# Products of ones, earlier matrix groups and later scoring in the graph layer of a graph-and-experts kernel

## The chip, the cores and the metric

The kernel runs on one NeuronCore of a Trainium2 chip. The core has five engines, each with its own queue that is worked off in order: TensorE (PE, matrix products and transposes), VectorE (DVE), ScalarE (ACT), GpSimd (POOL) and SyncE (SP, which here only starts transfers). Sixteen DMA engines move data between DRAM and the on-chip memory. The metric is the device time of one execution in microseconds (us).

## The reference

The input is x (1024 rows of 512, float32) and a list of 16384 edges sorted by their destination. Two layers follow:

```
h  = layernorm(x) @ W                      # 1024x512 @ 512x512
x  = x + relu(segment_sum(edge_weight * h[dst], src) + bias)
t  = layernorm(layernorm(x))               # two norms before the experts
scores = sigmoid(layernorm(x) @ Wg.T + bg) # 64 experts, the best 2 of each row
y  = sum over the 2 experts of weight * (silu(t W1' + b1') * (t W3' + b3')) @ W2 + b2
x  = x + y + shared_expert(t)
```

The graph layer's gather and sum over edges can be written as a product of a 1024x1024 matrix A (the summed edge weights) with h. The kernel does that.

## The kernel before

All of it is float32 with some bf16 helpers. A row tile is 128 rows, so there are NT = 8 tiles.

**Start (lines 219 to 331).** VectorE waits for the first edge of each partition (`first`, line 261), compares it with thresholds (`below`, 263), and TensorE counts the results in two small products (266). From the count VectorE gets the rows of the edge list that hold the block boundaries (268, 270), POOL loads them (273), and VectorE finds where each block of destinations starts (319 to 324). POOL then loads the windows of edges (331): destination, source and weight, and behind them on its queue the bias rows (`base_d`, 335), the small weights (`ws_raw`, 341, 342, and others) and the zeroing of `y_d` (372), whose source row is written by a memset on VectorE (371).

**Products with W.** `center(i)` is VectorE's mean of a tile and its subtraction. `turn_h(i)` is four transposes on TensorE (193) and a copy on ScalarE (300). `times_w(i)` is four products with W (307, each shown as two records) and a scaled copy on ScalarE (308) into `hws`. The order of these calls is written out by hand: TensorE, VectorE, ScalarE and POOL issue in the order of the program, except that some instructions behind the branch `tc.If(unsure)` (446) are placed ahead of it.

**Edge parts.** VectorE splits the loaded windows into parts (381 to 388). TensorE transposes the six parts (393 to 395), which stand behind `times_w(3)`, and VectorE copies the results (396, 399).

**One-hots and matrix groups.** The matrix A is made in two halves (h = 0, 1) of 8 groups each; I number the groups 0 to 15. `one_hots(h, g)` (401 to 421) is four steps on VectorE (408 three times, 419) and a cast on ScalarE (417). `matrix_group` (489 to 500) is 16 small products on TensorE (495) and two copies on ScalarE (500) into A. The one-hots run two groups ahead of the products. All groups stand behind `times_w(7)`. In the second half, each group is followed by `turn` (four transposes, 507, and a copy to AT, 508) and one or two products with h (`weighted_sum`, 514); by the end of the second half the first half's sums of tiles 0, 1 and 2 are done ahead (`NE3 = 3`).

**Tile loop (689 to 718).** In pass t the remaining products of tile t are run, `turn` is done for tile t + 2, and then four more steps stand one, two or three passes behind: `store_nx(t-1)` (ScalarE 545, POOL 546), `score_bias`, `turn_x` and `scores` of tile t-1 (TensorE 558, 193, 563; ScalarE 552, 566, 567), `choose`, `rank`, `put` and `slots` of tile t-2 (VectorE 572 to 611, TensorE 597, 599, POOL 620, 622) and `listed(t-3)` (TensorE 628). `finish(t)` closes the pass: VectorE adds the bias rows and x (529, 530), takes the norms (166, 167, 174 to 183) and writes the normalized row tile (187) and the shift (541).

The rows of one pass as they stand in the code:

```
for a in todo[:n0]: weighted_sum(*a)
turn(As[1], 1, t + 2); summed(t + 1); store_nx(t - 1); listed(t - 3)
for a in todo[n0:n1]: weighted_sum(*a)
score_bias(t - 1); turn_x(t - 1)
choose(t - 2); rank(t - 2); put(t - 2); slots(t - 2, ...)
for a in todo[n1:]: weighted_sum(*a)
scores(t - 1); finish(t)
```

**Experts (721 on).** From the lists (720) POOL gathers the rows of a pair of experts (752), TensorE transposes them (193) and multiplies them with the weights (781, 803), and POOL scatters the results (810). SyncE loads the weights of all 64 experts through two rings of 13 buffers; most of the graph layer's tiles are taken from the same rings.

## Time and profile before

| what | us |
|---|---|
| median of 4 runs (445.25 to 448.84) | 446.4 |
| profiled execution | 446.28 |
| its span, first to last instruction | 444.5 |
| first product with W starts | 9.94 |
| edge parts on TensorE start | 30.48 |
| matrix group 0 starts | 46.74 |
| first sum done, `finish(0)` starts | 92.08 |
| first gather of rows for an expert | 174.42 |

Busy time in the span: TensorE 394.3 us (89%), VectorE 244.0 (55%), ScalarE 117.3 (26%), GpSimd 121.9 (27%). A busy TensorE is not TensorE at its peak: its records overlap, and the clock that the throttle grants falls below 1.00 in some stretches. A row of the timeline gives start and duration in us, engine, line of the kernel, operation, output<-input, and a count; in brackets stands how long the engine was idle before it and what released it. Matrix products of float32 show as two records each.

### The profile page before, as it was taken

What the parts mean: (1) busy time and instruction counts of PE and PEld (TensorE: products, weight loads), DVE (VectorE), ACT (ScalarE), POOL (GpSimd) and SP (SyncE); (2) the same over time, 40 slices, a digit from 0 to 9 for tenths busy, and PEclk for the clock granted to TensorE, in tenths of its full rate; (3) what the DMA queues carried; (4) which work ended last, traced back from release to release, by engine and by line L of the source; (5) the groups of instructions that cost most, each with busy time, mean ns of one, the idle gap of its engine ahead of it and who ended that gap; (6) DMA issues with size and microseconds to landing.
All of it is one profiled execution on the core that took longest, in us unless ns stands there. A gap on an engine that the chain in (4) does not pass through costs nothing.

```text
span 444.5 us, 6426 instructions
## 1 busy us (share of the span) xinstructions
PE 394.3 (89%) x2130; PEld 186.9 (42%) x2130; DVE 244.0 (55%) x723; ACT 117.3 (26%) x241; POOL 121.9 (27%) x162
## 2 busy tenths in 40 slices
PE   2999769988999963799976999999999999999793
PEld 1554446645555542334422343444434434434241
DVE  4969899648777883422366353534424333331781
ACT  1235799432222221111201121221221212212100
POOL 5450800002333234232231141423231322313000
PEclk9999999988999975799998999999999999999898
DMA  8377492992534199379999999999999999999572
GB/s 261 99 112 104 126 358 103 406 375 67 171 119 160 51 383 370 124 233 414 407 406 407 408 408 406 408 409 408 405 409 408 406 408 406 406 409 375 220 279 89
DMA packets 40983, 132.50 MB, mean 298 GB/s; under 512 B 7116, under 2 KB 7260, under 8 KB 40816
## 3 DMA queue, kind: packets, MB, share of 16 engines
q1 hardware_dynamic: 31040, 109.66, 63.1%
q0 software_dynamic: 9184, 20.28, 15.7%
q10 hardware_dynamic: 720, 2.10, 1.2%
q8 instruction: 18, 0.29, 0.3%
q14 instruction: 21, 0.17, 0.1%
HBM read 124.13 MB, written 18.62 MB: 321 GB/s over the span
## 4 chain that ended last, share of the span: by engine, by line
PE 69%; DVE 8%; DMA 5%; ACT 4%; issue 2%; POOL 0%; POOLq 0%; ACTq 0%; DVEq 0%
PE xph L781 23%; PE xpy L803 12%; PE acc L514 12%; PE xpt L193 3%; DMA y_d<-xy,lists 3%; PE xph L777 2%; PE xpht L793 2%; ACT ov L417 2%; PE ph L495 2%; PE xpy L942 2%; PE ph L563 2%; PE pt L507 1%; PE pt L193 1%; DMA bw<-w_d,lists 1%; ACT A L500 1%
## 5 line engine op out<-in xcount | busy, mean ns | idle before, releaser
L781 PE MATMUL xph<-w,xT 128*64 128x512 f32 (+1 forms) x520 | 121.5, 596 | 0.1
L810 POOL DMA_INDIRECT y_d<-xy,lists x30 | 31.1, 1037 | 146.0 <-DMA y_d<-xy,lists 68.6
L803 PE MATMUL xpy<-w,xhT 128*64 128x512 f32 (+1 forms) x260 | 66.5, 614 | 4.7 <-ACT xhT L795 4.7
L781 PEld LDWEIGHTS xph<-w,xT 128*64 128x64 f32 (+1 forms) x520 | 38.6, 138 | 61.3 <-issue 57.6
L514 PE MATMUL acc<-hw,AT 128*128 128x512 f32 x128 | 62.5, 615 | 0.4 <-ACT AT L508 0.4
L786 DVE TENSOR_TENSOR xh<-xa,xph 128x256 f32<-128x256 f32 x33 | 13.9, 421 | 86.8 <-ACT xa L784 72.6
L784 ACT ACTIVATE xa<-xph 128x256 f32<-128x256 f32 x33 | 12.7, 385 | 114.8 <-PE xph L781 114.8
L752 POOL DMA_INDIRECT rows<-nx_d,tokens x32 | 34.7, 1083 | 15.7 <-issue 8.0
L803 PEld LDWEIGHTS xpy<-w,xhT 128*64 128x64 f32 (+1 forms) x260 | 19.7, 143 | 45.4 <-issue 38.3
L764 DVE TENSOR_TENSOR xT<-xpt,gT 128x512 f32<-128x512 f32 x32 | 22.1, 690 | 25.1 <-PE xpt L193 23.1
L806 ACT COPY xy<-xpy 128x512 f32<-128x512 f32 x33 | 19.4, 587 | 48.4 <-PE xpy L803 42.8
L307 PE MATMUL ph<-w_sb,hT 128*128 128x512 f32 x64 | 31.5, 640 | 0.7 <-ACT hT L300 0.7
L514 PEld LDWEIGHTS acc<-hw,AT 128*128 128x128 f32 x128 | 22.6, 195 | 17.3 <-issue 16.7
L193 PE MATMUL xpt<-ident,rows 128*128 128x128 f32 x132 | 22.0, 293 | 4.8 <-DMA rows<-nx_d,tokens 4.8
L546 POOL DMA_DIRECT2D nx_d<-row x8 | 4.5, 563 | 76.8 <-ACT row L545 76.8
L417 ACT CAST ov<-eq 128x1536 f32<-128x1536 bf16 x16 | 24.8, 1553 | 0.0
L766 DVE TENSOR_TENSOR xT<-xT,bT 128x512 f32<-128x512 f32 x32 | 22.1, 692 | 1.1
L495 PE MATMUL ph<-ov,ol 128*32 128x128 f32 x512 | 17.4, 276 | 5.4 <-ACT A L500 5.0
L193 PEld LDWEIGHTS xpt<-ident,rows 128*128 128x128 f32 x132 | 19.2, 211 | 5.0 <-DMA rows<-nx_d,tokens 4.9
L793 PEld LDWEIGHTS xpht<-ident,xh 128*128 128x128 f32 x66 | 11.7, 210 | 19.7 <-DVE xh L786 10.7
L193 PE MATMUL pt<-ident,row 128*128 128x128 f32 x64 | 12.4, 322 | 8.3 <-DVE row L187 2.8
L793 PE MATMUL xpht<-ident,xh 128*128 128x128 f32 x66 | 14.7, 305 | 4.9 <-DVE xh L786 4.9
(271 smaller groups left out, 505.7 us busy)
## 6 DMA issues: line engine op xcount, KB each, us to landing
w<-in_L_ffn_W_dram SPq DMA_DIRECT2D x195, 512.0 KB
y_d<-row POOLq DMA_DIRECT2D x1, 4096.0 KB
ys<-y_d SPq DMA_DIRECT2D x8, 512.0 KB
base_d<-in_L_gnn_bias_dram POOLq DMA_DIRECT2D x1, 2048.0 KB
row<-base_d POOLq DMA_DIRECT2D x8, 256.0 KB
nx_d<-row POOLq DMA_DIRECT2D x8, 256.0 KB
w_sb<-in_L_gnn_W_dram ACTq DMA_DIRECT2D x1, 1024.0 KB
res<-in_x_dram SPq DMA_DIRECT2D x2, 512.0 KB
```

Source lines behind the costliest of these rows:

```text
L193: nc.tensor.transpose(ps[:, k, :], v[:, k, :], ident[:n, :n])
L307: nc.tensor.matmul(ph, hT[:, k, :], w_sb[:, k, :], start=(k == 0), stop=(k == KC - 1))
L417: nc.scalar.copy(ov[:, :, :VA], eq)
L495: nc.tensor.matmul(pa[LO * w:LO * (w + 1), u, :], ol[:, q, :], ov[:, q, :], start=True, stop=True)
L514: nc.tensor.matmul(accs[t], ATs[h][t // 4][:, t % 4, wq, :], hws[h][:, wq, :], start=(h == 0 and wq == 0), stop=(h == NH - 1 and wq == NQ ...
L752: nc.gpsimd.indirect_dma_start(out=rows, out_offset=None, in_=nx_d[:, :], in_offset=bass.IndirectOffsetOnAxis(ap=of, axis=0), bounds_check ...
L764: nc.vector.tensor_tensor(xT.rearrange(view, n=n), pt.rearrange(view, n=n), g[:, :, :, None].to_broadcast(over), ALU.mult)
L766: nc.vector.tensor_tensor(xT.rearrange(view, n=n), xT.rearrange(view, n=n), b[:, :, :, None].to_broadcast(over), ALU.add)
L781: nc.tensor.matmul(ph[n * r:(n + 1) * r], xT[:, k, n * r:(n + 1) * r], w13[:, :, k, :], start=False, stop=(k == KC - 1))
L793: nc.tensor.transpose(pt[:, c, :], v[:, c, :], ident)
L803: nc.tensor.matmul(py[n * r:(n + 1) * r], hT[:, c, n * r:(n + 1) * r], w2[:, c, :], start=(c == 0), stop=(c == HC - 1))
L810: nc.gpsimd.indirect_dma_start(out=y_d[:, :], out_offset=bass.IndirectOffsetOnAxis(ap=numbers, axis=0), in_=y, in_offset=None, bounds_chec ...
```

## The change

It has three parts.

1. **Products of ones.** A helper `keep_warm(n)` multiplies the bf16 tile `ones_b` with itself into an accumulator that nobody reads. Nine such products stand ahead of the two counting products, six behind them, and two behind `turn_h(0)`.
2. **Groups among the products with W.** Three of the sixteen matrix groups are moved ahead of the branch: group 0 behind `times_w(5)`, group 1 behind `times_w(6)`, group 2 behind `times_w(7)`. Their one-hots move up with them, from where on one-hots run one group ahead instead of two. The transposes of the edge parts move into the middle of `times_w(3)`. The zero row is written by ScalarE instead of VectorE. The count of edges inside the windows (`sm`, `inside`) moves behind the one-hots of group 1.
3. **Scoring of the first three tiles.** Tile 0 is scored in pass 2 instead of pass 1, tiles 1 and 2 both in pass 3 (before: passes 2 and 3). The choice follows one pass later (tile 0 in pass 3, tiles 1 and 2 in pass 4), the lists again one pass later (pass 4, and both in pass 5). From tile 3 on nothing changes. The rings of `so` and `bo` have 6 buffers instead of 4.

```diff
+            def keep_warm(n):
+                pz = psc.tile([P, D], F32, name="acc")
+                for _ in range(n):
+                    nc.tensor.matmul(pz, ones_b, ones_b[:, None, :].to_broadcast([P, D // P, P]), start=True, stop=True)
...
+            keep_warm(9)
             pn = psh.tile([P, D], F32, name="ph")
             for h in range(NH):
                 nc.tensor.matmul(pn[:, h:h + 1], below[:, h, :], ones_b[:, 0:1], start=True, stop=True)
+            keep_warm(6)
...
             for k in range(KC):
+                if k == KC // 2 and amid:
+                    amid()
                 nc.tensor.matmul(ph, hT[:, k, :], w_sb[:, k, :], start=(k == 0), stop=(k == KC - 1))
...
             turn_h(0)
+            keep_warm(2)
...
-            nc.vector.memset(zero, 0.0)
+            nc.scalar.activation(zero, ones[:, 0:1].to_broadcast([P, D]), AF.Copy, scale=0.0)
...
             turn_h(4)
-            times_w(3)
...
+            times_w(3, turn_parts)
...
             turn_h(5)
+            ohs[0] = one_hots(0, 0)
             times_w(4)
             turn_h(6)
-            times_w(5)
+            ohs[1] = one_hots(0, 1)
...
+            times_w(5)
+            matrix_group(As[0], 0, 0, ohs.pop(0))
...
             turn_h(7)
+            ohs[2] = one_hots(0, 2)
             times_w(6)
+            matrix_group(As[0], 0, 1, ohs.pop(1))
+            ohs[3] = one_hots(0, 3)
             times_w(7)
+            matrix_group(As[0], 0, 2, ohs.pop(2))
...
-                    so = rt.tile([P, P], F32, name="so", bufs=4)
+                    so = rt.tile([P, P], F32, name="so", bufs=6)
...
-            for g in range(8):
-                ohs.append(one_hots(0, g + 2) if g + 2 < 8 else one_hots(1, g + 2 - 8))
-                matrix_group(As[0], 0, g, ohs.pop(0))
-                if g == 1:
+            for g in range(3, 8):
+                ohs[g + 1] = one_hots(0, g + 1) if g + 1 < 8 else one_hots(1, 0)
+                matrix_group(As[0], 0, g, ohs.pop(g))
+                if g == 3:
...
-                if have(3):
-                    listed(t - 3)
+                scored, chosen, put_down = (
+                    ([], [0], [1, 2])[t - n] if n <= t < n + 3 else [t - n] if have(n) else [] for n in (1, 2, 3))
+                for c in put_down:
+                    listed(c)
+                if len(scored) == 2:
+                    score_bias(scored[0])
+                    turn_x(scored[0])
                 for a in todo[n0:n1]:
                     weighted_sum(*a)
-                if have(1):
-                    score_bias(t - 1)
-                    turn_x(t - 1)
-                if have(2):
-                    choose(t - 2)
-                    rank(t - 2)
-                    put(t - 2)
-                    slots(t - 2, nc.vector if t - 2 == NT - 1 else nc.gpsimd)
+                if len(scored) == 2:
+                    scores(scored.pop(0))
+                for c in scored:
+                    score_bias(c)
+                    turn_x(c)
+                for c in chosen:
+                    choose(c)
+                    rank(c)
+                    put(c)
+                    slots(c, nc.vector if c == NT - 1 else nc.gpsimd)
                 for a in todo[n1:]:
                     weighted_sum(*a)
-                if have(1):
-                    scores(t - 1)
+                for c in scored:
+                    scores(c)
```

The scaling of the shared expert's weights (636, VectorE) keeps its place by group: it stood behind the one-hots of group 3 and now stands behind those of group 4.

## The prediction

> **What bounds the kernel now.** I read the page's busy line first, then the chain of waits, then the timelines of TensorE, VectorE and ScalarE in the first 145 us, where all edits lie. TensorE is busy for 394.3 of 444.5 us. Behind 145 us every step hangs on the lists made from the scores, and the weight loads wait for buffers that the same steps free, so I count time won before 145 us as time won at the end.

> The early stage, from the timeline (start, duration, engine, line, what, count, in brackets idle time before and its releaser):

> ```profile
> 9.94 6.31 PE L307 MATMUL ph<-w_sb,hT 128*128 128x512 f32 x8 [0.68 <-ACT hT L300]
> 19.23 3.60 PE L307 MATMUL ph<-w_sb,hT 128*128 128x512 f32 x8
> 27.04 3.60 PE L307 MATMUL ph<-w_sb,hT 128*128 128x512 f32 x8
> 30.48 0.27 PE L393 MATMUL acc<-ident,windows 128*128 128x128 f32 x1
> 51.27 1.08 PE L495 MATMUL ph<-ov,ol 128*32 128x128 f32 x32 [0.84 <-ACT A L500]
> 63.16 1.08 PE L495 MATMUL ph<-ov,ol 128*32 128x128 f32 x32
> ```
> ```profile
> 24.93 0.48 DVE L371 MEMSET row<- 128x512 f32 x1
> 31.22 1.22 DVE L396 CAST values<-acc 128x1024 bf16<-128x1024 f32 x1 [3.21 <-PE acc L394]
> 44.74 0.43 DVE L636 TENSOR_TENSOR wall<-ws_raw,gs_sb 128x256 f32<-128x256 f32 x1 [0.26 <-DMA ws_raw<-in_L_ffn_Ws_dram]
> ```

> The first product with W takes 6.31 us, the later ones 3.60: TensorE starts slowly. VectorE waits 3.21 us for the transposed edge parts, which stand behind times_w(3). From 51.27 a matrix group comes every 1.92 us, paced by ScalarE (cast 1.37 plus copies 0.55); from 63.16 TensorE itself paces.

> The tile loop, from the timelines, and granted clock by stretch (columns: stretch, length, busy time of PE, PEld, DVE, ACT, POOL, granted clock, DMA share, GB/s):

> ```profile
> 92.08 0.69 DVE L529 TENSOR_TENSOR row<-row,acc 128x512 f32<-128x512 f32 x1 [6.79 <-PE acc L514]
> 97.35 0.15 DVE L541 SCALAR_TENSOR_TENSOR mrs<-mvr,rs 128x1 f32<-128x1 f32 x1
> ```
> ```profile
> 97.58 1.10 PE L193 MATMUL pt<-ident,row 128*128 128x128 f32 x4 [2.11 <-DVE mrs L541]
> 105.89 0.72 PE L193 MATMUL pt<-ident,row 128*128 128x128 f32 x4 [1.03 <-issue]
> 107.23 0.19 PE L597 MATMUL ph<-chosen,before_b 128*128 128x64 bf16 x1 [0.62 <-ACT hT L552]
> ```
> ```profile
> 97.60:100.40 2.80, 2.80 (x8) 1.74 (x8) 0.00 (x0) 2.42 (x3) 1.08 (x2) 0.50 0.95 376
> 107.20:110.70 3.50, 3.47 (x11) 2.47 (x12) 2.79 (x11) 0.03 (x1) 2.24 (x5) 0.53 0.23 80
> ```

> finish(0) holds VectorE from 92.08 to 97.50 (5.42 us), and TensorE waits 2.11 us for its row, then 1.03 and 0.62. After such waits it runs at a clock of 0.50 for about 3 us.

> **Part 1, products of ones.** 17 bf16 products of 128x512. No row has one; the bf16 products at 117.88 and 117.91 (64 columns) start 0.03 us apart, so I take 8 x 0.03 = 0.24 us at full clock, 0.48 at half. The bound above is a whole f32 record of the same width when cold, 6.31/8 = 0.79; below, L777 starts two in 0.24, 0.12 each. Nine from 1.15 (ones_b written) end at 5.5, when the start search's products are due. Six after them end at 7.2 to 8.6; turn_h(0) stands at 8.16 now, so up to 0.5 is lost if they run slowly. Two lie beside the 0.59 us copy of hT. At 0.79 the nine would end at 8.3 and hold back L268 and all VectorE behind it by 2.7 us, of which its idle 0.41 and 1.33 cover 1.7: then 1 us is lost.
> If they warm the clock, times_w(0) falls from 6.31 to about 3.4 and ends by 13.4. ScalarE must then wait for rsx (VectorE, 14.36) before copying hw(0), then hT(1), wall, gT (0.69+0.58+0.37+0.37); turn_h(2) follows at 16.4 and times_w(1) at 17.0 instead of 19.23: 2.2 won there. Half a warm-up gives the same, since 14.36 ends last.
> [...]

> **Part 2, three groups earlier.** The memset leaves VectorE (0.40 to the next start) for ScalarE, which idles 2.5 us there; the nearest row, L1010, costs 0.56 each. Its user, the zeroing DMA on POOL, stays behind base_d's landing. VectorE's parts thus end at 27.6, not 28.0. TensorE has half of times_w(3) done at 26.7, turns the parts by 27.9 and finishes them plus the second half (1.72) at 29.7, against 31.13 now. The cast L396 starts at 28.0 instead of 31.22.
> From 29.7 TensorE needs: turn_h(5) to (7) and times_w(4) to (7), 3 x 0.57 + 4 x 3.43, three groups at 1.03 and the count's 0.14, 18.7 in all: 48.5, and 0.4 for the branch as now (the idle at 47.96): group 3 at 48.9 instead of 51.27. The casts of groups 3 and 4 stand before the branch on ScalarE, so group 4 follows at once, and from group 3's copies on (50.0) five steps of 1.92 lead to group 9 (the second half's second) at 59.7, against 63.16. The wait of 0.41 for the first AT behind it is gone too: group 10 starts at 62.3 instead of 66.36. I take **4.0 us**.
> VectorE's cover: its groups 0 to 4 end at 43.1, then it waits for ws_raw, which landed at 44.74, since base_d's load, ahead of it in POOL's queue, is not moved. Behind that come the branch (0.7) and 11 groups at 2.54: it ends at 73.7, not 76.5, and its cast input for group 9 at 56.8, 1.4 us before ScalarE wants it. If that cover goes, each us beyond 1.4 is lost.

> **Part 3, scoring later.** Everything 4.0 earlier, finish(0) runs 88.1 to 93.5. Tiles 1 and 2 need few products (1.72 + 0.45 + 1.72 before tile 1 is summed, at 91.8), so VectorE does finish(1) to 98.9 and finish(2) to 104.3 without pause. TensorE goes on with tile 2, score_bias(0) and turn_x(0) and is at scores(0) at 96.6. But ScalarE issues store_nx(1) before the copy of hT(0), and store_nx(1) needs finish(1): 98.9 + 0.75 + 0.59 = 100.3. **New wait: 3.7 us**; queued behind it are tile 3's products.
> Then scores 0.9 and pass 3 with two tiles (8 products 6.9, turn 0.45, twice bias, turn, scores 0.4+0.57+0.9, rank 0.05): 112.3. Pass 4 reaches rank(1) 7.2 later, 119.5. rank(2) follows it in TensorE's queue, but choose(2) stands behind put(1) on VectorE: 1.1 + 1.35 us: **second wait, 2.6 us**, with four products and scores(3) behind it. Pass 5 starts at 124.8 and, with one more pair of list products (0.38), ends at 135.1 against 140.40 now. At full clock that is 5.3 us won, 1.3 of it by this part.
> Both waits are as long as or longer than the 2.11 us after which 2.8 us ran at 0.50. I charge 1.4 each, **2.8**. Bounds: 0 to 1.75 each by the rows above (3.5 at 0.53), more if the low clock lasts on. DMA order, row buffers and the wider rings of so and bo cost nothing: base rows load 10 us ahead, and POOL's 2.35 us per tile for the two tiles ends at 126, before the lists at 129.
> [...]

> **Sum.** 4.0 + 1.3 - 2.8 = 2.5. The profiled execution took 446.28 (span 444.5 and 1.8 around it), 0.1 below the median of 446.4. Forecast **443.8 us**.

> **Rivals.**
> A. The clock stays up through the waits: 2.8 comes back, gain 5.3, **441.0**. For: 51 to 59 us ran at 1.00 with TensorE 56% busy. Against: both rows at half clock.
> B. The ones don't warm the clock (the change doesn't do what it says): times_w(0) stays at 6.31, the parts are turned at 29.4 and all behind is 1.7 later: gain 0.8, **445.5**. For: the first 6 us of work are slow now. Against: 3.8 us or more of added work.
> C. Slower: the low clock after the two waits. The new waits sum to 6.3 us, against 3.8 removed. If each is followed by two stretches of 3.5 us at half clock, it costs 2 x 3.5 = 7.0, not 2.8: 446.3 + 1.7 = **448.0**. It turns the sign where the clock's loss passes 5.3. Against: each stretch ended after 2.8 to 3.5 us.
> D. The front's gain is lost on the way, because the expert loop doesn't start earlier (its first weights come late): 446.3. Against: TensorE's first wait there is for gathered rows, not weights.

> **How the numbers follow.** Forecast 0.46, A 0.24, B 0.14, C 0.10, D 0.06. 1% is 4.5 us, about what a measurement of this kernel can tell from no change. Faster by more holds A and a part of the forecast, where less than 0.8 is lost to the clock: 0.27. Slower by over 1% needs C in an extreme form or something unseen: 0.08. The range reaches from under A (441.0, less 1 for an earlier end of the waits) to between B and C: 440.0 to 447.2.

> **What would show it.** Right: the second product with W near 17 us, the cast of L396 at about 28, group 10 at 62 to 63; a wait of 3 to 4 us before the first score products and of 2 to 3 us before the second rank of pass 4, both followed by a granted clock near 0.5; the gather of the first rows 2 to 3 us before 174.42. Wrong: a times_w(0) still over 6 us, those waits missing, or an expert loop of another length than now.

## The result: 0.4% slower

The changed kernel takes 447.93 us (median of 52 executions, 443.65 to 449.79), the kernel before 445.71 (78 executions, 442.48 to 449.95). The ratio is 1.0039, with a 95% interval of 1.0026 to 1.0051: 1.2 to 2.3 us slower. (The ratio is an estimate of its own; the quotient of the two medians is 1.0050.) The forecast was 443.8, its range ended at 447.2. The profiled execution of the changed kernel took 450.12 us (span 448.4), 2.2 over its median and above the highest of the 52, so it is a late one of its kind.

TensorE's timeline in the first 65 us of the changed kernel:

```profile
1.21 4.02 PE L224 MATMUL acc<-ones_b 128*128 128x512 bf16 x9 [1.21 <-DVE ones_b L123]
9.76 3.70 PE L317 MATMUL ph<-w_sb,hT 128*128 128x512 f32 x8 [0.24 <-ACT hT L308]
16.14 1.23 PE L193 MATMUL pt<-ident,raw 64*128 64x64 f32 x8 [1.59 <-ACT hT L308]
18.27 4.43 PE L317 MATMUL ph<-w_sb,hT 128*128 128x512 f32 x8
26.90 1.88 PE L317 MATMUL ph<-w_sb,hT 128*128 128x512 f32 x4
28.62 0.27 PE L405 MATMUL acc<-ident,windows 128*128 128x128 f32 x1
50.27 1.96 PE L443 MATMUL ph<-ov,ol 128*32 128x128 f32 x64 [0.33 <-PEq L480]
61.15 1.08 PE L443 MATMUL ph<-ov,ol 128*32 128x128 f32 x32 [0.19 <-ACT ov L431]
```

The ones do speed up the first products with W: times_w(0) lasts 3.70 instead of 6.31. It does so in all ten profiles with the ones that follow, and takes 5.35 to 6.63 in the four without. But TensorE is then ahead of ScalarE, waits 1.59 us for a copy, and times_w(1) behind it takes 4.43 instead of 3.60. The parts are turned from 28.62 (before 30.48; the forecast had them done by 27.9), group 3 runs at 50.27 (before 51.27, forecast 48.9), group 9 at 61.15 (63.16, 59.7).

VectorE's timeline:

```profile
29.37 1.23 DVE L410 CAST values<-acc 128x1024 bf16<-128x1024 f32 x1 [1.45 <-PE acc L406]
89.38 0.69 DVE L550 TENSOR_TENSOR row<-row,acc 128x512 f32<-128x512 f32 x1 [7.27 <-PE acc L535]
94.73 0.68 DVE L550 TENSOR_TENSOR row<-row,acc 128x512 f32<-128x512 f32 x1
100.07 0.68 DVE L550 TENSOR_TENSOR row<-row,acc 128x512 f32<-128x512 f32 x1
```

finish(0), (1) and (2) follow each other without pause, as forecast, and finish(0) starts 2.7 us earlier than before (92.08). The two new waits of the tile loop, on TensorE, and what ScalarE does ahead of the first:

```profile
101.52 1.81 PE L584 MATMUL ph<-wall,hT 128*128 128x128 f32 x8 [3.32 <-ACT hT L573]
125.44 0.20 PE L618 MATMUL ph<-chosen,before_b 128*128 128x64 bf16 x1 [2.50 <-DVE chosen L600]
```
```profile
100.19 0.81 ACT L566 ACTIVATE row<-res,mrs,rs 128x512 f32<-128x512 f32 x1 [3.95 <-DVE mrs L562]
100.91 0.56 ACT L573 COPY hT<-pt 128x512 f32<-128x512 f32 x1
```

Both waits are there, at the places forecast and nearly as long: 3.32 (3.7) and 2.50 (2.6). ScalarE stands at the store of tile 1's row (L566) for 3.95 us, and the copy of hT(0) behind it. By finish(7), at 158.41 against 158.59, of the 2.7 us that finish(0) had won 0.2 are left.

### The profile page after: what moved, and what is told of

It reads as the page before. It is cut to its first block, busy times and chain, and to the rows that moved or that the text cites. A ratio compares the mean times of both kernels' runs of the same rounds, so it can differ in the third digit from the quotient of the medians.

```text
span 448.4 us, 6462 instructions
## 1 busy us (share of the span) xinstructions
PE 400.8 (89%) x2147; PEld 188.1 (42%) x2147; DVE 243.6 (54%) x722; ACT 117.5 (26%) x242; POOL 120.8 (27%) x162
## 4 chain that ended last, share of the span: by engine, by line
PE 54%; DMA 17%; DVE 9%; issue 4%; ACT 3%; POOL 0%; POOLq 0%; ACTq 0%; DVEq 0%
PE xph L809 15%; DMA y_d<-xy,lists 14%; PE acc L535 11%; PE xpy L831 9%; PE xpt L193 2%; PE ph L584 2%; PE ph L443 2%; PE pt L528 2%; PE xpht L821 2%; DMA y_d<-xy,lists_o 1%; PE xph L805 1%; PE pt L193 1%; ACT ov L431 1%; PE xpy L937 1%; DMA bw<-w_d,lists 1%
## 5 line engine op out<-in xcount | busy, mean ns | idle before, releaser
L831 PE MATMUL xpy<-w,xhT 128*64 128x512 f32 (+1 forms) x260 | 67.5, 622 | 4.8 <-ACT xhT L823 4.8
L317 PE MATMUL ph<-w_sb,hT 128*128 128x512 f32 x64 | 30.0, 609 | 0.2 <-ACT hT L308 0.2
L193 PE MATMUL xpt<-ident,rows 128*128 128x128 f32 x132 | 22.0, 293 | 5.0 <-DMA rows<-nx_d,tokens 5.0
L193 PEld LDWEIGHTS xpt<-ident,rows 128*128 128x128 f32 x132 | 19.3, 211 | 5.1 <-DMA rows<-nx_d,tokens 5.1
L443 PEld LDWEIGHTS ph<-ov,ol 128*32 128x32 f32 x512 | 13.1, 109 | 12.6 <-ACT ov L431 6.7
```

The costliest lines, as they stand in the source:

```text
L193: nc.tensor.transpose(ps[:, k, :], v[:, k, :], ident[:n, :n])
L317: nc.tensor.matmul(ph, hT[:, k, :], w_sb[:, k, :], start=(k == 0), stop=(k == KC - 1))
L443: nc.tensor.matmul(pa[LO * w:LO * (w + 1), u, :], ol[:, q, :], ov[:, q, :], start=True, stop=True)
L831: nc.tensor.matmul(py[n * r:(n + 1) * r], hT[:, c, n * r:(n + 1) * r], w2[:, c, :], start=(c == 0), stop=(c == HC - 1))
```

## The experiments

One quantity carries most of what follows: the tile loop from the start of finish(0) to the start of finish(7). It is 66.5 us in the profile before and 69.0 in the changed kernel. A "low stretch" is a stretch at a granted clock of 0.50. Every one that I measured in steps of 0.1 us is 3.4 us long, or a multiple of it, so by estimate one costs 1.7 us of TensorE's work (half of 3.4; a run below takes two of them away and wins 3.4).

| kernel | finish(0) | loop | low stretches in the loop | median us | ratio to before (95%) |
|---|---|---|---|---|---|
| before | 92.08 | 66.5 | 2 | 445.71 | |
| before, second profile | 91.83 | 65.3 | 1 | | |
| changed | 89.38 | 69.0 | 2 | 447.93 | 1.0039 (1.0026 to 1.0051) |
| part 1 alone | 90.60 | 63.7 | 1 | 445.86 | 1.001 (0.998 to 1.004) |
| part 2 alone | 90.99 | 65.3 | 1 | 445.27 | 0.9998 (0.9969 to 1.0027) |
| part 3 alone | 92.60 | 69.0 | 2 | 449.82 | 1.0109 (1.0073 to 1.0145) |
| parts 1 and 2 | 89.53 | 64.6 | 1 | 444.18 | 0.995 (0.992 to 0.998) |
| changed, ones in the two waits | 90.15 | 65.7 | 0 | 445.74 | 0.9996 (0.9972 to 1.0019) |
| changed, first wait gone | 89.83 | 65.1 | 1 | 443.14 | 0.994 (0.992 to 0.997) |
| changed, second wait gone | 89.25 | 65.6 | 1 | 445.05 | 0.9955 (0.992 to 0.999) |
| changed, both waits gone | 88.23 | 61.7 | 0 | 442.07 | 0.990 (0.986 to 0.993) |
| parts 1 and 2, ones ahead of the rows | 88.40 | 64.7 | 1 | 442.51 | 0.991 (0.9885 to 0.994) |
| both waits gone, ones ahead of the rows | 89.51 | 61.7 | 0 | 439.75 | 0.985 (0.981 to 0.9885) |
| the same and ones in the front's wait | 88.62 | 61.7 | 0 | 439.04 | 0.985 (0.9815 to 0.988) |

The first three numbers of a row are from one profiled execution each; the medians and ratios are from 5 to 78 executions, each ratio against executions of the kernel before on the same chip.

### The parts alone

Part 1 alone (only the three calls of `keep_warm`):

> The kernel before with part 1 alone (the products of ones). My theory after reading the changed kernel's trace: the ones warm the clock (times_w(0) lasts 3.7 us instead of 6.31), but TensorE then waits 1.6 us for ScalarE and falls to half clock, so that the end of times_w(1) comes only 0.1 us earlier (22.7 instead of 22.8); part 1 is worth 0 to 0.2 us, ratio 0.999 to 1.000. Rival, the prediction's own count: 2.2 us won at times_w(1) and carried to the end, ratio 0.995.

times_w(1) starts at 17.8 (before 19.2, in its second profile 19.0), and finish(0) 1.2 to 1.5 us earlier, in a profile that has no low stretch in the front. The time doesn't move. Nine profiles here have the ones and nothing in TensorE's wait behind them, which is 1.48 to 1.95 us long in eight of them and 0.51 in one. In six of the nine a low stretch follows, at 16 to 22 us. By estimate, a gain of 1.35 less two thirds of 1.7 leaves 0.2 us on the mean, which the ratio's interval (0.9 us won to 1.8 lost) holds.

Part 2 alone (the edge parts inside times_w(3), the zero row, the three groups):

> The kernel before with part 2 alone (edge parts turned inside times_w(3), zero row on ScalarE, three groups among the last products with W). If the front's gain is part 2's and carries to the end: group 10 at 63.7 to 63.9 instead of 66.36, 2.5 us won, ratio 0.994. Rival: the gain is there at group 10 but is lost behind 145 us, since the later stages do not start earlier or pay it back: ratio 0.998 to 1.002. Second rival: without the ones the group's start falls back, gain 1.5 at group 10.

The parts are turned from 27.97 without any ones, 2.5 us earlier, but finish(0) comes only 0.8 to 1.1 earlier. On TensorE this profile has a pause in the middle of group 4:

```profile
53.27 2.15 PE L440 MATMUL ph<-ov,ol 128*32 128x128 f32 x51 [2.03 <-issue]
```

Nothing that the profile shows ends this wait of 2.03 us, and no other profile here has it. Two low stretches in a row follow, at 54.4 to 61.2, and from group 3 to group 10 it takes 15.5 us, where the changed kernel takes 13.4. The ratio shows no gain; its interval reaches to 1.4 us.

Part 3 alone (the loop's new order and the wider rings):

> The kernel before with part 3 alone (the first three tiles scored one tile later). The changed kernel's trace shows 2.7 us won at group 10 and 0.2 left at the start of the sixth pass, so part 3 costs 2.5 us in the tile loop: two waits of 3.3 and 2.5 us, with a clock of 0.5 to 0.6 behind each; the sixth pass starts at 142.9, ratio 1.0056. Rival: part 3 costs nothing in itself and the changed kernel's loss arises behind 174 us: sixth pass at 140.4, ratio 1.000.

The loop takes 69.0 us, the changed kernel's, with the same two waits (3.32 and 2.49). Part 3 by itself costs 3.3 to 6.5 us, more than the 2.5 that the two first profiles had shown.

Parts 1 and 2 together:

> The changed kernel without part 3. If part 3 is what loses the time, this wins 2.7 us at group 10 and keeps it: sixth pass at 137.7, ratio 0.994, and it beats both kernels. Rival: the expert stage does not carry time won ahead of it (the clock after the wait for the first gathered rows, the order of the last transfers): sixth pass at 137.7 but ratio 0.999 to 1.003. Parts add: this should be e1 and e2 together.

This is 0.8 to 3.6 us faster than the kernel before: some of what the front wins (2.55 at finish(0)) does reach the end, and the rival that the expert stage swallows all of it falls. That it swallows a part does not: from finish(7) to the end of the span the profiles take 285.9 to 287.2 us in the five that have at most one of parts 1 and 2, and 288.1 to 291.0 in the six that have both and no ones ahead of the rows (a profile or two of each kernel). No run takes this difference apart. From here to the changed kernel (0.995 to 1.0039) only part 3 is added: 4.0 us. Why parts 1 and 2 win together and show nothing each stays half open: for the ones the low stretch explains it, for part 2 alone there is one profile with a pause and two low stretches, which is no rate.

### Why part 3 costs more than the two profiles showed

The kernel before was profiled once more, unchanged:

> The kernel before, a second look. Its first profile has two low stretches of 1.7 us in the tile loop (97 to 101 and 107 to 111 us); the three kernels with the same loop that ran since have one. If the second is a matter of chance, this profile has one, and the loop from finish(0) to finish(7) takes about 64.8 us instead of 66.5; part 3 then starts from a better loop than the prediction took. Rival: it is the kernel's own, 66.5 again.

The loop is 65.3 us, with one low stretch. Windows of the two profiles of the same kernel (columns: window, length, busy time of TensorE, of its weight load, of VectorE, ScalarE and GpSimd, each with its count, granted clock, DMA share, GB/s). The first profile:

```profile
93.72:97.13 3.41, 1.76 (x9) 0.81 (x7) 2.92 (x16) 0.69 (x1) 0.00 (x0) 1.00 0.91 321
97.13:100.55 3.42, 2.97 (x8) 1.93 (x9) 0.50 (x3) 2.63 (x3) 1.08 (x2) 0.50 0.94 371
103.96:107.37 3.41, 1.76 (x10) 1.02 (x9) 2.99 (x18) 1.68 (x3) 0.37 (x1) 1.00 0.00 0
107.37:110.79 3.42, 3.42 (x12) 2.39 (x12) 2.69 (x9) 0.00 (x0) 2.16 (x5) 0.50 0.23 81
```

The second:

```profile
93.05:96.46 3.41, 2.18 (x10) 0.98 (x8) 2.93 (x16) 0.69 (x1) 0.00 (x0) 1.00 0.92 336
96.46:99.87 3.41, 2.53 (x15) 1.92 (x16) 1.64 (x5) 2.56 (x3) 1.08 (x2) 1.00 0.99 360
103.29:106.70 3.41, 1.71 (x8) 1.08 (x8) 3.07 (x17) 1.34 (x2) 0.54 (x1) 1.00 0.03 11
106.70:110.11 3.41, 3.41 (x11) 2.38 (x10) 3.13 (x12) 0.33 (x2) 2.78 (x5) 0.50 0.20 71
```

The windows are not arbitrary. Within one execution the low stretches start on a grid: in the changed kernel at 16.5, 101.8, 125.7, 163.3 and 238.4 us, the later four 25, 32, 43 and 65 steps of 3.414 us behind the first. In each of the other 13 profiles a grid of 3.412 to 3.4145 us can be laid through the starts (those before 250 us) to within 0.03 us on the mean. The windows above are this grid. In both profiles TensorE waits the same 2.11 us for mrs. In the first, 1.65 of a window's 3.41 us are idle, and the next window runs at half clock. In the second the grid lies 0.4 us earlier against the wait (it began 1.75 us into a window, and now 2.18), the wait is split over two windows (1.23 and 0.88 idle), and the clock stays up.

The same count over all 14 profiles, from 16 to 250 us, of windows that are not low themselves: of 38 with 2.0 us or more idle, all 38 are followed by a low one; of 33 with 1.5 to 2.0, 10; of 55 with 1.0 to 1.5, one; of 701 with less, none. Between 1.5 and 2.0 the idle time alone does not decide: 1.65 us was followed by a low window in the loop above, 1.68 by none among the matrix groups. Outside this range the idle time within a grid window told, in all cases but one, whether a low stretch followed. So it matters where the grid lies, and that was not the same in two executions of one kernel (0.4 us apart against the wait in the two profiles above).

Idle time was not the whole measure. Ahead of 16 us one profile (second wait gone) has a low window behind one with only 0.51 us idle, 13.42 to 16.83; but behind the product with W that ends at 14.0 TensorE did only transposes in it. Whether that is why the next window was low, no run tried by itself. In the five other profiles with a low stretch there, 1.48 to 1.64 us of the window before it were idle, again with transposes in it; in the three without one, 1.28 us at most.

The old loop stands in six profiles, each with the wait of 2.11 (2.10 in two); the waits of 1.03 and 0.62 vary, and with part 1 alone neither is over 0.5. It takes 66.5, 65.3, 63.7, 65.3, 64.6 and 64.7, a mean of 65.0, with two low stretches once and one five times (behind the wait of 2.11 in three profiles, behind the others in two). The profile that I predicted from is the worst of the six. The new waits, left unfilled, never slipped through:

```profile
98.41:101.82 3.41, 0.30 (x2) 0.30 (x3) 3.13 (x11) 1.61 (x3) 0.53 (x1) 1.00 0.17 66
101.82:105.24 3.42, 3.42 (x11) 2.32 (x10) 2.93 (x16) 1.28 (x3) 0.55 (x2) 0.50 0.45 153
122.31:125.72 3.41, 0.91 (x9) 0.79 (x10) 2.47 (x14) 0.58 (x1) 1.55 (x3) 1.00 0.21 79
125.72:129.14 3.42, 3.42 (x6) 1.36 (x6) 1.35 (x9) 0.00 (x0) 2.54 (x6) 0.50 0.00 0
```

That is the changed kernel: 3.11 and 2.50 us idle in a window, each followed by a low one. Each wait is in three profiles (the changed kernel, part 3 alone, and the kernel with the other wait taken away), and all six times a low stretch follows.

### The waits and the clock taken apart

Products of ones in the waits, which stay:

```diff
                 for c in chosen:
                     choose(c)
+                    if c == 2:
+                        fill(9)
                     rank(c)
...
+                if t == 2:
+                    fill(12)
                 for c in scored:
                     scores(c)
```

`fill(n)` is `keep_warm(n)` into one of the accumulators `pt`.

> The changed kernel with products of ones in its two new waits (12 ahead of the scores of tile 0, 9 ahead of the rank of tile 2; the waits stay). If it is the clock behind the waits that costs, the clock stays at 1.00 behind both, two low stretches of 1.7 us each go, ratio 0.996 to 0.998. If the waits themselves cost, the loop from finish(0) to finish(7) stays 2.5 us above the 63.1 us that the kernel before has with its low stretches taken off, and the ratio stays above 1. Rival: the clock does not hang on the waits and the ratio is the changed kernel's 1.004.

TensorE's timeline:

```profile
98.81 2.75 PE L580 MATMUL pt<-ones_b 128*128 128x512 bf16 x12
102.29 1.16 PE L591 MATMUL ph<-wall,hT 128*128 128x128 f32 x8 [0.73 <-ACT hT L573]
121.87 2.11 PE L580 MATMUL pt<-ones_b 128*128 128x512 bf16 x9
124.53 0.20 PE L625 MATMUL ph<-chosen,before_b 128*128 128x64 bf16 x1 [0.55 <-DVE chosen L607]
```

The clock is 1.00 through the loop, which falls from 69.0 to 65.7: 3.4 us, two low stretches. That is the clock's share of part 3. What is left is the waits': the old loop without its low stretches is 62.0 to 63.6 us (each profile less 1.7 for each stretch), so 65.7 is 2.1 to 3.7 too long. The waits' difference is 3.32 + 2.50 - (2.11 + 1.03 + 0.62) = 2.1. The time comes back to that of the kernel before, 1.9 us of the 3.4 by the medians' ratios; the intervals (1.0026 to 1.0051, 0.9972 to 1.0019) hold the 3.4 too.

Then the waits themselves were taken away, each by moving what it waits for:

```diff
-                if have(1):
+                if have(1) and t != 2:
                     store_nx(t - 1)
...
                 for c in scored:
                     score_bias(c)
                     turn_x(c)
+                if t == 2:
+                    store_nx(1)
-                for c in chosen:
+                for c in chosen[:1]:
                     choose(c); rank(c); put(c); slots(c, ...)
                 for a in todo[n1:]:
                     weighted_sum(*a)
+                for c in chosen[1:]:
+                    choose(c); rank(c); put(c); slots(c, ...)
```

> The changed kernel with the two new waits taken away: in the second pass the storing of tile 1's row stands behind the copy of hT(0) on ScalarE, and tile 2 is chosen and ranked behind the pass's last four products. If the two waits (3.3 and 2.5 us) and the clock that falls behind them are what part 3 costs, the tile loop from finish(0) to finish(7) is 5 us or more shorter than the changed kernel's 69.0, and the kernel is at 440 to 443 us, ratio 0.985 to 0.993, better than without part 3 (444.2). Rival: VectorE, which does three finishes back to back and each choose behind them, is the bound and only passes the wait on: loop over 67 us, ratio 0.998 to 1.004.

```profile
105.70 1.16 PE L584 MATMUL ph<-wall,hT 128*128 128x128 f32 x8 [0.98 <-ACT hT L573]
120.36 0.20 PE L618 MATMUL ph<-chosen,before_b 128*128 128x64 bf16 x1 [0.70 <-DVE chosen L600]
```

Those two are the waits left of over 0.5 us; no window of the loop is low, the loop is 61.7 us, and the kernel is 0.7 to 1.4% faster than the kernel before. VectorE was not the bound. (That is 3.0 to 6.2 us, where the front's 2.7 and a loop of 61.7 in place of 65.0 sum to 6.0: the whole may reach the end, or half of it.) Each wait by itself:

> The changed kernel with only the first of the two waits taken away (the storing of tile 1's row behind the copy of hT(0) on ScalarE). With both away the loop from finish(0) to finish(7) was 61.7 us and the ratio 0.990. Each wait priced by itself: the first 3.3 us and a low stretch of 1.7 us behind it, less 1.0 that the next pass waits instead: 4.0 us off the changed kernel's 69.0, loop 65.0, ratio 0.995. Rival: the first wait only moves to the second (rank(2) then waits longer for VectorE), loop over 67.5 and ratio over 1.000.

> The changed kernel with only the second wait taken away (tile 2 chosen and ranked behind the pass's last four products). By itself the second wait is worth 2.5 - 0.7 us and a low stretch of 1.7, 3.5 us in all: loop from finish(0) to finish(7) 65.5, ratio 0.996. Rival: the clock's stretch stays without it, 1.8 us, ratio 1.000.

The loops are 65.1 and 65.6, so the first wait is worth 3.9 us and the second 3.4, in sum the 7.3 of both (69.0 to 61.7). A wait of 2.50 us of which 1.8 can go is thus worth 3.4.

### The same remedy elsewhere

Ones behind the last product of the list, where TensorE waits for the first gathered rows, in the kernel with parts 1 and 2:

```diff
+            fill(12)
             nc.vector.tensor_scalar(lists, plist, float(PAD), None, op0=ALU.add)
```

> The changed kernel without part 3, with 12 products of ones behind the list's last product, where TensorE waits 5 us for the first gathered rows. If the low clock of the first expert unit (0.50 to 0.83 from 173 to 188 us) costs time, 1.7 to 3.4 us are won: ratio 0.987 to 0.991 against 0.995 without the ones. Rival: that stretch is covered by the transfers behind it (the weights that TensorE waits for at 225 to 240 us), ratio 0.995.

TensorE's timeline without these ones (parts 1 and 2):

```profile
173.32 1.98 PE L193 MATMUL xpt<-ident,rows 128*128 128x128 f32 x8 [5.00 <-DMA rows<-nx_d,tokens]
175.95 4.42 PE L801 MATMUL xph<-w,xT 128*64 128x512 f32 x16
```

and with them:

```profile
167.13 5.31 PE L580 MATMUL pt<-ones_b 128*128 128x512 bf16 x12
172.49 1.28 PE L193 MATMUL xpt<-ident,rows 128*128 128x128 f32 x8
174.80 3.72 PE L809 MATMUL xph<-w,xT 128*64 128x512 f32 x16 [0.69 <-DVE xT L794]
```

The first transposes fall from 1.98 to 1.28 us and the first expert products from 4.42 to 3.72. The ratio goes from 0.995 to 0.991, as expected, but the intervals (0.992 to 0.998, 0.9885 to 0.994) overlap, so that the times alone do not show this step.

Together with the waits taken away:

> Both waits taken away, and 12 products of ones in the wait for the first gathered rows. If the two gains add (0.990 and the 1.7 us of the ones), ratio 0.986, 439.5 us. Rival: the transfers limit the expert stage, so that what is won ahead is given back at the waits for weights: ratio 0.989 to 0.991.

The ratio is 0.985 (0.981 to 0.9885), 439.75 us: the gains add, and the rival's 0.989 to 0.991 lies outside. Last, the same with six ones more in the front, behind the first of the three sets of rows that are turned there:

```diff
                 nc.scalar.copy(to, pt[:, :, :E])
+                if raw is by_expert[0]:
+                    keep_warm(6)
```

> As the last, with 6 more products of ones in the 1.6 us in which TensorE waits for ScalarE between the first two transposes of the gate's rows. Three of six traces with the ones in front have a low stretch of 1.7 us right behind that wait, at 16 to 22 us. If the wait causes it, none is seen there now and 0.5 to 1 us is won on the mean, ratio 0.984 to 0.986. Rival: the low stretch stays, ratio as without, 0.986.

TensorE's timeline:

```profile
14.48 1.47 PE L224 MATMUL acc<-ones_b 128*128 128x512 bf16 x6
16.20 1.17 PE L193 MATMUL pt<-ident,raw 64*128 64x64 f32 x8 [0.26 <-ACT hT L308]
17.94 3.60 PE L317 MATMUL ph<-w_sb,hT 128*128 128x512 f32 x8
```

In this profile no low stretch follows, and times_w(1) takes 3.60. Its grid lies within 0.01 us of that of the run before, so the same two windows can be compared, first without and then with the six ones:

```profile
13.50:16.91 3.41, 1.93 (x15) 1.67 (x14) 3.03 (x15) 1.59 (x4) 0.68 (x1) 1.00 0.06 20
16.91:20.33 3.42, 3.42 (x10) 2.09 (x10) 3.28 (x8) 1.18 (x3) 2.50 (x4) 0.50 0.16 38
13.50:16.92 3.42, 3.16 (x20) 2.01 (x19) 3.04 (x15) 1.44 (x3) 0.51 (x1) 1.00 0.09 28
16.92:20.33 3.41, 3.41 (x14) 2.04 (x14) 3.23 (x9) 1.33 (x3) 2.50 (x4) 1.00 0.16 38
```

In this pair, filling the wait (1.48 us idle without the ones, 0.26 with them) kept the clock up. The ratio is the same as without (0.985), so the gain of 0.5 to 1 us is neither shown nor excluded. At 439.04 and 439.75 us these two are 1.1 to 1.9% faster than the kernel before, and the fastest here.

## Why the prediction was wrong

**The first part of the change** was right in its mechanism: the ones speed up the first products with W (3.70 us for 6.31; rival B falls), and ScalarE's wait for rsx then ends last. Not priced was that this leaves TensorE idle for 1.6 us, and that a low stretch follows where 1.48 us or more of it lie in one window (five profiles; none in the three with 1.28 us at most). times_w(1) starts at 17.7 to 18.3, not 17.0. With part 1 alone it is 17.84 without any low stretch: rsx is ready at 14.78, not 14.36, and two of the three sets of gate rows (1.17 us of transposes, from 16.10) stand on TensorE ahead of turn_h(2); the sum left these transposes out. The price of a product of ones, 0.24 us at full clock and 0.48 at half, was right (0.23, and 0.44 at a granted clock of 0.50: the 12 in 5.31 us ahead of the first gathered rows).

**The front's 4.0 us** were mis-sized, for the most part by that low stretch. In the two profiles in which the grid lay well (both waits gone, and parts 1 and 2 with ones ahead of the rows) finish(0) is at 88.23 and 88.40: 3.85 and 3.7 won, nearly the forecast. In the changed kernel it is 2.7, with a low stretch at 16.5 to 19.9; the mean of the eight profiles with this front unaltered is 89.3, 2.8 won. Of this lead little is left behind the loop: the first gather of rows starts at 174.16, 0.3 us earlier than before, where the forecast had 2 to 3.

**The tile loop** is where the sign was lost. Both waits stood where the prediction put them and at nearly its lengths (its two terms for the second, 1.1 and 1.35, sum to 2.45, not 2.6; 2.50 was measured). The step that failed is "at full clock that is 5.3 us won, 1.3 of it by this part". The 1.3 compared a new loop at full clock with an old one that held the two low stretches of the profile before, 3.4 us, as if both were the old loop's own. Without them part 3 loses 2.1 at full clock: waits of 5.8 in place of 3.8. In five of six profiles the old loop has one such stretch, not two, so 1.7 of the gain wasn't there to be had.

**The clock's loss of 2.8** was too small: a stretch is 3.4 us long and costs 1.7, two cost 3.4. The 1.4 came from windows that I had cut by eye.

With the measured terms: the front -2.7, the loop 69.0 - 65.0 = +4.0, in sum +1.3; measured is +1.2 to +2.3. Against the one profile before, the loop's term is only +2.5.

**The rivals.** C named the mechanism and the side, but its price was wrong: it asked for two low stretches behind each wait. One behind each is enough, once the old loop is taken at its mean. A falls: the clock did not stay up behind either wait in any profile where the wait was left unfilled. D falls in its full form: with parts 1 and 2 alone, 0.8 to 3.6 us reach the end; whether a part is lost in the expert stage stays open. Between the two first profiles the whole difference of 3.9 us in the spans (448.4 against 444.5) lies behind finish(7); that the loss comes from the tile loop rests on the old loop's mean and on the runs that change the loop alone.

## What to carry to other kernels

Take the low-clock stretches out of the old schedule before you price a new one: those of one profile may be the luck of that execution (two in the loop in the first profile of the kernel before, one in the second), and a second profile of the unchanged kernel costs little. Here a wait of TensorE cost its length and, where it filled 2 us or more of one 3.4 us window, 1.7 us more; products that nobody reads saved the second part (the loop fell from 69.0 to 65.7 us), but only moving the awaited step saved both (61.7). When steps are moved later, look at what stands ahead of what they need on the queues of the other engines: here the waits of 3.32 and 2.50 us fell to 0.98 and 0.70 by moving one store and one choice.
